# Cross-attention on one core: the rest of A of the last group by block products in one long step, and three pieces of row work on ScalarE

## The chip, the core and the metric

The kernel runs on one core of a Trainium2 chip, in float32. The engines of a core work side by side, each through its own list of instructions in the order written: TensorE (PE, matrix products, with its weight loads PEld), VectorE (DVE), ScalarE (ACT), GpSimd (POOL) and SyncE (SP, which here issues the transfers). They wait for each other by semaphores. The metric is the device time of one execution in microseconds (us): before the change 269.1 us, the median of three runs (268.92 to 269.33).

## The reference

Sixteen batches of 256 rows `x` (256 wide) attend to 77 rows of a context `c` (192 wide) with 8 heads of width 256; then comes a projection, the residual and a layer norm:

```python
Q = (img_embed @ Wq).reshape(B, -1, H, D).transpose(0, 2, 1, 3)
K = (sent_embed @ Wk)...; V = (sent_embed @ Wv)...      # as Q
score = jnp.einsum('bhqd,bhkd->bhqk', Q, K) / math.sqrt(D)
attn = jax.nn.softmax(jnp.where(mask, score, -jnp.inf), axis=-1)
ctx = jnp.einsum('bhqk,bhkd->bqhd', attn, V).reshape(B, -1, H * D)
out = ctx @ Wo + img_embed
mu = jnp.mean(out, axis=-1, keepdims=True)
var = jnp.var(out, axis=-1, keepdims=True)
return (out - mu) * jax.lax.rsqrt(var + EPS) * gamma + beta
```

## The kernel before, in words

**What is computed in which order.** The kernel never forms Q, K or V. For each head it first forms G = Wk'Wq (and U = Wv Wo), from the weights alone. Then A = G'c of a batch (256 x 77 per head) is what the rows of x are multiplied with for the scores, and VW = U'c of a batch is what the attention weights are multiplied with for the output. Batches stand in four groups of four (`GB`); A is held by group in `a_of[g]`, for all 8 heads. Each batch has two tiles of 128 rows, 32 tiles in all; tiles 2b and 2b+1 belong to batch b.

**Two ways to A.** `prepare_a` (L178) forms it directly: for a place (a pair of heads) and two or four batches, 32-column products over 128 rows of c (`part_A`, L203) and over the 64 rows that are left (`part_B`, L215); the results are copied by ACT. `prepare_fast` (L278) forms it for a pair of heads and four batches of a group by 11 block products in place of 12: 64 x 64 products (L361) on sums of blocks of G (`gS`, `gC`) and c (`cT`, `cD`) that were made earlier; ACT copies one block a head (L370), and `put_together` adds the rest on DVE, four additions a head (L373).

**The work on a tile.** `scores` (PE, L469), `shift` (DVE, L486: mask, and the maximum for each head), `exponential` (ACT, L512, eight heads one after the other; with `summed_by_act` ACT also sums each head's row, which costs a read of an accumulator a head, and otherwise DVE sums them in `weigh`, L525), `weigh` (DVE reciprocal L527, POOL multiplication L533), `turn` (DVE transposition L543). Then a batch's output: `seven` (PE, L622: seven block products over both tiles, with sums of the weights `sums` and of VW `differences` made on POOL, and ACT's copy of the products, L647), `add_seven` (DVE L676 and POOL L664, into x), and for the last batches `attend` and `attend_halves` (PE L555, L571). At last the layer norm: `finish` (statistics of the row: by two ACT passes L687 and L688 if `by_act`, otherwise by DVE L691 and L692), `spread` (the reciprocal deviation on ACT, L710 and L711), `normalise` (DVE L731 and L760) and `store` (SP).

**The steps.** The order is written out by hand; each engine takes its instructions in just that order. Batches go in two kinds of steps. A `long_step(b)` takes the scores of batch b+1, `seven(b)`, VW of two batches and two `prepare_fast` calls (one half of a group's heads), and later shifts, turns and normalisations; `short_step(b)`, for the next batch, has only scores, `seven` and what goes with them. They alternate from b = -1 up to `ready`, here 9: long steps at -1, 1, 3, 5 and 7. Work that a step leaves over stands in the list `behind` (the last additions of `put_together`, normalisations) and is done in the next one. From `ready` on come ordinary steps for b = 9 to 14 (the loop before the last lines): scores of b+1, `work_of` of one or two batches (VW, and with it A), exponentials, statistics of batch b-1, `seven(b)` up to b = 12, `attend` after that. In this text "the stage of 9 and 10" is the two steps with b = 9 and b = 10, and so on.

**A of the last group.** Group 3 (batches 12 to 15) gets heads 0 to 3 by `prepare_fast` in the long step of batch 7. Heads 4 to 7 come in the ordinary steps: `work_of` of batches 10, 11, 12 and 13 each adds one `prepare_a` for one pair of heads and two batches, between the products of VW.

**Queues and buffers.** SP issues the loads of x (`load_x`), of its columns (`load_xT`) and the stores, in order. PSUM has eight buffers (`ps_mm`), handed out in turn, which every product's result takes and an ACT or DVE instruction frees.

Of the kernel before, what the change touches and what calls it, by code (L numbers as in the profile page):

```python
# [20 lines left out]
GB = 4  # L21
# [6 lines left out]
def kernel(  # L28
# [14 lines left out]
    B, S, DI = x.shape  # L43
# [3 lines left out]
    NG = B // GB  # L47
    QT = S // P
    NT = B * QT
    GT = GB * QT  # L50
    NF = H // 2
# [40 lines left out]
    def flat(ap):  # L92
        return ap.rearrange("p a b -> p (a b)")
# [10 lines left out]
    NS = B - GB // 2 - 1  # L104
# [23 lines left out]
    def half(i):  # L128
        return slice(i * LB, (i + 1) * LB)
# [21 lines left out]
    def in_two(name, shape, g):  # L151
        return pools[g % 2].tile(shape, F32, tag=f"{name}{g % 2}", name=f"{name}_{g}", bufs=1)
# [25 lines left out]
    def prepare_a(g, places, lo=0, hi=GB, rest_first=False):  # L178


        if 0 in places:
            a_of[g] = in_two("a", [P, 2, GB, H, S2], g)
        parts = [
            (2 * u + i, dc) for u in places for dc in range(2) for i in range(2)
        ]
        batches = slice(g * GB + lo, g * GB + hi)
        each = GB // (hi - lo)
        whole = [
            ps_mm.tile([P, each, hi - lo, S2], F32, tag="mm", name=f"pa_{g}_{h}_{dc}_{lo}")
            for h, dc in parts[: len(parts) // each]  # L190
        ]
        banks = [w[:, i] for i in range(each) for w in whole]
        opening, closing = range(len(whole)), range(len(parts) - len(whole), len(parts))

        def cols(dc, i):
            return slice(dc * P + i * BK, dc * P + (i + 1) * BK)

        wide = 2 if len(places) == 1 and g == 0 else 1

        def part_A():  # L200
            for n, ((h, dc), o) in enumerate(zip(parts, banks)):
                for i in range(NM):
                    nc.tensor.matmul(  # L203
                        flat(o[i * BK : (i + 1) * BK]),
                        gA[:, h, cols(dc, i)],
                        flat(cA[:, batches, :]),
                        start=not rest_first and n in opening,
                        stop=rest_first and n in closing,
                    )

        def part_B():
            for j in range(0, len(parts), 2):
                for i in range(0, NM, wide):
                    for k, (h, dc) in enumerate(parts[j : j + 2]):
                        nc.tensor.matmul(  # L215
                            flat(banks[j + k][i * BK : (i + wide) * BK]),
                            gB[half(k), h // 2, dc * P + i * BK : dc * P + (i + wide) * BK],
                            flat(cB[half(k), batches, :]),
                            start=rest_first and j + k in opening,
                            stop=not rest_first and j + k in closing,  # L220
                        )

        def copies():
            return [(a_of[g][:, dc, lo:hi, h, :], o) for (h, dc), o in zip(parts, banks)]

        return part_A, part_B, copies
# [157 lines left out]
    def prepare_vw(b, rest_first=False):  # L384

        vw_of[b] = vwp.tile([P, 4, 2, P], F32, tag="vw", name=f"vw_{b}", bufs=3)
        parts = slice(0, 4) if b < NS else slice(1, 5)
        pv = [ps_mm.tile([P, 2 * DI], F32, tag="mm", name=f"pv_{b}_{k}") for k in range(2)]

        def part_A():  # L390
            for k in range(2):
                for i in range(NM):
                    nc.tensor.matmul(  # L393
                        pv[k][i * BK : (i + 1) * BK],
                        cA[:, b, k * BK : (k + 1) * BK],
                        uA[:, parts, :, i],
                        start=not rest_first,
                        stop=rest_first,
                    )

        def part_B():
            for i in range(NM):
                for k in range(2):
                    nc.tensor.matmul(  # L404
                        pv[k][i * BK : (i + 1) * BK],
                        cB[half(k), b, k * BK : (k + 1) * BK],
                        uB[half(k), parts, :, i],
                        start=rest_first,
                        stop=not rest_first,
                    )  # L410

        def copies():
            return [
                (vw_of[b][:, :, k, :], pv[k].rearrange("p (q d) -> p q d", q=4)) for k in range(2)
            ]

        return part_A, part_B, copies
# [78 lines left out]
        s_of[t] = s, top  # L496

    def by_act(t):
        return t // QT < B - 2 * GB - 1

    def fast(b):
        return b < B - GB - GB // 2

    def summed_by_act(t):
        return not QT * NS <= t < NT - QT

    def exponential(t):
        s, top = s_of.pop(t)
        den = st.tile([P, H], F32, tag="den", name=f"den_{t}")
        for h in range(H):  # L510
            one = slice(h, h + 1)
            nc.scalar.activation(  # L512
                s[:, h],
                s[:, h],
                AF.Exp,
                bias=top[:, one],
                scale=-1.0,
                accum_out=den[:, one] if summed_by_act(t) else None,
            )
        e_of[t] = s, den  # L520

    def weigh(t):
        e, den = e_of.pop(t)
        if not summed_by_act(t):
            nc.vector.tensor_reduce(den, e, AX.X, ALU.add)  # L525
        rden = st.tile([P, H], F32, tag="rden", name=f"rden_{t}")
        nc.vector.reciprocal(rden, den)  # L527
        p = p_ring[t % 2]
        e_mh = e.rearrange("p (m h) k -> p m h k", h=2)
        rden_mh = rden.rearrange("p (m h) -> p m h", h=2)  # L530
        for cols, keys in ((slice(2 * KM), slice(KM)), (slice(2 * KM, 2 * S2), slice(KM, None))):
            part = p[:, :, cols].rearrange("p m (h k) -> p m h k", h=2)
            nc.gpsimd.tensor_tensor(  # L533
                part,
                e_mh[:, :, :, keys],
                rden_mh.unsqueeze(3).to_broadcast(list(part.shape)),
                ALU.mult,
            )
# [139 lines left out]
    def finish(t):  # L678
        if t in po_of:
            add_product(t)  # L680
        g, j = t // GT, t % GT
        y = x_of(t)[:, 0, :]
        if j == 0:
            mv_of[g] = st.tile([P, GT, 2], F32, tag="mv", name=f"mv_{g}", bufs=2)
        if by_act(t):
            mean, var = (mv_of[g][:, j, n : n + 1] for n in range(2))
            nc.scalar.activation(junk, y, AF.Identity, scale=1.0 / DI, accum_out=mean)  # L687
            nc.scalar.activation(junk, y, AF.Square, bias=mean, scale=-1.0, accum_out=var)  # L688
            return
        bn = st.tile([P, 6], F32, tag="bn", name=f"bn_{t}")  # L690
        nc.vector.bn_stats(bn, y)  # L691
        nc.vector.bn_aggr(mv_of[g][:, j, :], bn)  # L692
# [12 lines left out]
    def spread(first, last):  # L705

        g, lo, hi = first // GT, first % GT, (last - 1) % GT + 1
        log = st.tile([P, GT], F32, tag="log", name=f"log_{first}")
        rstd = st.tile([P, GT], F32, tag="rstd", name=f"rstd_{first}")
        nc.scalar.activation(log[:, lo:hi], mv_of[g][:, lo:hi, 1], AF.Ln, bias=eps, scale=1.0 / DI if by_act(first) else 1.0)  # L710
        nc.scalar.activation(rstd[:, lo:hi], log[:, lo:hi], AF.Exp, scale=-0.5)  # L711
        all_rstd_of[first, last] = rstd
# [424 lines left out]


    def work_of(b, rest_first=False):
        g, n = b // GB + 1, b % GB  # L1140
        work = [prepare_vw(b, rest_first)]
        if b <= NS and not fast(b):
            part = (0, 2) if g < NG else (2, GB)
            work.append(prepare_a(NG - 1, (NF // 2 + n % 2,), *part, rest_first))
        return work

    def copy_out(work):
        for _, _, copies in work:
# [40 lines left out]
    def long_step(b):  # L1189
# [10 lines left out]
        for m in range(0, 2) if b < 0 else range(b + 2, min(b + 3, B // 2)):  # L1200
            turn_last(m)
        works = work_of(b + 1) + work_of(b + 2)
        for part_A, *_ in works:
            part_A()
# [71 lines left out]

        between.append(last_turn)

    ready = B - GB - GB // 2 - 1
    for b in range(-1, ready, 2):  # L1280
        long_step(b)
        short_step(b + 1)
# [2 lines left out]
    for b in range(ready, B - 1):  # L1285
# [6 lines left out]
        g, n = (b + 1) // GB + 1, (b + 1) % GB  # L1292
# [116 lines left out]
```

## Time and profile before

| | before |
|---|---|
| median of 3 runs | 269.1 us (268.92 to 269.33) |
| the profiled execution | 268.58 us, of which the span of the instructions is 266.8 us |
| TensorE busy, granted clock | 260.5 us (98%), 1.00 |
| VectorE / ScalarE / GpSimd busy | 212.7 / 166.9 / 191.5 us (80 / 63 / 72%) |
| last product of TensorE ends | 262.0 us after the start of the span |
| DMA | 22.73 MB, mean 85 GB/s |

Times in the profile are counted from the start of the span of one profiled execution. A row of a group reads: line, engine, operation, what it writes and reads, its shape, how often | busy us, mean ns of one | idle time of the engine before them, and what ended it. A row in order of time reads: start, length, engine, line; an idle time before it stands in brackets with what ended it. A row of waits reads: who waited for whom: us in total, how often, the longest. A row of the chain reads: start, length, what. Matrix products overlap, so the end of a row of PE is later than the next one's start.

### The profile page before, as it was taken

How to read it: one execution, taken by the hardware profiler on the slowest of the kernel's cores; microseconds unless marked ns; L12 is line 12 of the kernel's file. 1: busy time of each engine (PE TensorE's matmuls, PEld its weight loads, DVE VectorE, ACT ScalarE, POOL GpSimd, SP SyncE). 2: the span in 40 equal slices, each digit the busy share in tenths (PEclk: the TensorE clock that was granted, in tenths of full speed). 3: DMA queues.
4: the chain of work that ended last, by engine and by line, in shares of the span. 5: the costliest groups of instructions: out<-in, count | busy, mean ns of one | idle time of the engine just before them, and what ended most of it. 6: DMA issues, size and time to landing. Idle time of an engine off the chain costs nothing.

```text
span 266.8 us, 15067 instructions
## 1 busy us (share of the span) xinstructions
PE 260.5 (98%) x6330; PEld 202.8 (76%) x6330; DVE 212.7 (80%) x860; ACT 166.9 (63%) x710; POOL 191.5 (72%) x272
## 2 busy tenths in 40 slices
PE   7999999999999999999999999999999999999992
PEld 6566578948986899679967996799669957985662
DVE  0554968479893789988997969898988798799785
ACT  3253548624584689648983798467964595636772
POOL 1042098799459896899479996997699899685452
PEclk9999999999999999999999999999999999999999
DMA  6999997900240002131314012221234010100112
GB/s 188 209 206 225 335 148 160 300 18 4 63 104 5 2 6 66 58 90 37 83 43 122 5 24 65 81 85 41 54 127 132 20 44 2 44 23 25 42 43 80
DMA packets 41699, 22.73 MB, mean 85 GB/s; under 512 B 24144, under 2 KB 40608, under 8 KB 41632
## 3 DMA queue, kind: packets, MB, share of 16 engines
q1 hardware_dynamic: 41248, 20.98, 31.3%
q0 software_dynamic: 384, 0.79, 1.3%
q8 instruction: 50, 0.82, 1.3%
q14 instruction: 17, 0.14, 0.2%
HBM read 17.57 MB, written 4.19 MB: 82 GB/s over the span
## 4 chain that ended last, share of the span: by engine, by line
PE 96%; DMA 2%; DVE 1%; SPq 0%; issue 0%; DVEq 0%
PE ps L469 25%; PE pf L361 11%; PE po L622 11%; PE pv L393 10%; PE pm L622 9%; PE pv L404 6%; PE pa L203 5%; PE po L555 4%; PE pu L956 3%; PE pa L215 2%; PE pr L429 2%; PE pgb L1017 2%; DMA wq_nat<-in_L_xattn_Wq_dram 2%; PE pw L970 1%; PE pr L440 1%; PE phb L1033 1%
## 5 line engine op out<-in xcount | busy, mean ns | idle before, releaser
L512 ACT ACTIVATE s<-s,top 128x77 f32<-128x77 f32 x256 | 85.2, 346 | 24.5 <-DVE top L486 24.5
L469 PE MATMUL ps<-a,xT 128*32 128x154 f32 x2048 | 70.1, 294 | 0.0
L469 PEld LDWEIGHTS ps<-a,xT 128*32 128x32 f32 x2048 | 65.8, 110 | 2.0 <-issue 1.5
L533 POOL TENSOR_TENSOR p<-s,rden 128x512 f32<-128x512 f32 x64 | 47.7, 769 | 21.9 <-DVE rden L527 21.7
L486 DVE CUSTOM_DVE_ANT_0 s<-ps,bias 128x77 f32<-128x77 f32 x256 | 43.3, 232 | 4.6 <-PE ps L469 4.0
L512 ACT ACTIVATION_READ_ACCUMULATOR s<-s,top 128x1 f32 x224 | 41.9, 187 | 0.0
L373 DVE TENSOR_TENSOR a<-pf,a 128x154 f32<-128x154 f32 x80 | 33.9, 435 | 7.3 <-PE pf L361 4.9
L664 POOL TENSOR_TENSOR xg<-xg,m 128x256 f32<-128x256 f32 x39 | 28.8, 738 | 2.7 <-DVE xg L676 0.7
L543 DVE STREAM_TRANSPOSE pT<-p 128x640 f32<-128x640 f32 x32 | 26.3, 827 | 5.1 <-POOL p L533 5.0
L393 PE MATMUL pv<-uA,cA 128*32 128x512 f32 x256 | 29.6, 593 | 0.0
L1150 ACT COPY vw<-pv 128x512 f32<-128x512 f32 x32 | 17.1, 587 | 14.9 <-PE pv L404 14.9
L760 DVE SCALAR_TENSOR_TENSOR xg<-xg,rstd,bet 128x256 f32<-128x256 f32 x27 | 22.7, 840 | 2.6 <-ACT rstd L711 1.2
L586 POOL TENSOR_TENSOR ts<-vw 128x768 f32<-128x768 f32 x13 | 23.6, 1831 | 0.0
L486 DVE DVE_READ_ACCUMULATOR2_ANT top<- 128x1 f32 x256 | 20.9, 82 | 0.0
L393 PEld LDWEIGHTS pv<-uA,cA 128*32 128x32 f32 x256 | 8.0, 110 | 13.3 <-issue 9.8
L731 DVE SCALAR_TENSOR_TENSOR xg<-xg,mv,gam 128x256 f32<-128x256 f32 x30 | 18.0, 600 | 0.1
L361 PE MATMUL pf<-cT,gS 64*64 64x154 f32 x240 | 17.4, 290 | 0.0
L603 POOL TENSOR_TENSOR ss<-pT 128x256 f32<-128x256 f32 x13 | 9.7, 745 | 9.8 <-DVE pT L543 9.7
L404 PE MATMUL pv<-uB,cB 64*32 64x512 f32 x256 | 16.3, 596 | 0.0
L622 PE MATMUL po<-vr,pT 128*32 128x256 f32 x208 | 16.0, 379 | 0.0
L361 PEld LDWEIGHTS pf<-cT,gS 64*64 64x64 f32 x240 | 15.8, 133 | 0.0
L203 PE MATMUL pa<-cA,gA 128*32 128x308 f32 (+1 forms) x256 | 14.0, 360 | 0.0
(153 smaller groups left out, 543.1 us busy)
## 6 DMA issues: line engine op xcount, KB each, us to landing
xg<-in_x_dram SPq DMA_DIRECT2D x8, 512.0 KB, 4.4
xT<-in_x_dram SPq DMA_DIRECT2D x56, 64.0 KB, 2.7
out_dram<-xg SPq DMA_DIRECT2D x11, 256.0 KB, 2.7
wo<-in_L_xattn_Wo_dram SPq DMA_DIRECT2D x4, 512.0 KB, 7.9
wq_blk<-in_L_xattn_Wq_dram SPq DMA_DIRECT2D x12, 128.0 KB, 4.6
out_dram<-xg SPq DMA_DIRECT2D x10, 128.0 KB, 1.7
wk_blk<-in_L_xattn_Wk_dram SPq DMA_DIRECT2D x12, 96.0 KB, 4.0
wvT<-in_L_xattn_Wv_dram POOLq DMA_DIRECT2D x8, 96.0 KB, 6.3
```

The lines of the kernel that those rows point to most:

```text
L203: nc.tensor.matmul(flat(o[i * BK : (i + 1) * BK]), gA[:, h, cols(dc, i)], flat(cA[:, batches, :]), start=not rest_first and n in opening, ...
L361: nc.tensor.matmul(bank[half(i), n], weight(i), moving, start=start, stop=stop,)
L373: nc.vector.tensor_tensor(out, *of, ALU.add)
L393: nc.tensor.matmul(pv[k][i * BK : (i + 1) * BK], cA[:, b, k * BK : (k + 1) * BK], uA[:, parts, :, i], start=not rest_first, stop=rest_first,)
L404: nc.tensor.matmul(pv[k][i * BK : (i + 1) * BK], cB[half(k), b, k * BK : (k + 1) * BK], uB[half(k), parts, :, i], start=rest_first, stop=n ...
L469: nc.tensor.matmul(ps[m // 2][i * BK : (i + 1) * BK, m % 2 * 2 * S2 : (m % 2 + 1) * 2 * S2], xT_of[t // PT][:, j * NM + m, dc], flat(a_of[ ...
L486: nc.vector.tensor_tensor_reduce(s[:, h], ps[a][:, k * S2 : (k + 1) * S2], bias[:, b, :], scale=-1.0, scalar=FAR, op0=ALU.add, op1=ALU.min ...
L512: nc.scalar.activation(s[:, h], s[:, h], AF.Exp, bias=top[:, one], scale=-1.0, accum_out=den[:, one] if summed_by_act(t) else None,)
L533: nc.gpsimd.tensor_tensor(part, e_mh[:, :, :, keys], rden_mh.unsqueeze(3).to_broadcast(list(part.shape)), ALU.mult,)
L543: nc.vector.transpose(pT_of[t].rearrange("p n m q -> p m n q"), p.rearrange("p m (n k) -> p m n k", k=BK),)
L622: nc.tensor.matmul(out[i * BK : (i + 1) * BK], weight[:, i], moving, start=first and n == 0, stop=final and n == len(terms) - 1,)
L664: nc.gpsimd.tensor_tensor(to, to, what, ALU.add)
```

## The change

Three lines of conditions and a list are changed, and with them the steps that exist:

- `ready` becomes 11, so that batches 9 and 10 also go by a long step and a short step. The long step of batch 9 calls `prepare_fast` for the pairs of heads 2 and 3 (heads 4 to 7) of group 3, all four batches, 88 products of 64 x 64. The ordinary steps are then b = 11 to 14.
- `work_of` no longer calls `prepare_a`; `fast` is gone. In the ordinary steps b = 9 and b = 11 this removes two calls each.
- `by_act(t)` holds for batches below 9 (before: below 7), so the statistics of batches 7 and 8, four tiles, are two ACT passes a tile in place of DVE's.
- `summed_by_act(t)` leaves out batch 14 alone (before: 13 and 14), so ACT sums the exponentials of batch 13's two tiles.
- The loads of x for batches 14 and 15, which stood in the ordinary step b = 9, now stand in the long step.

```diff
@@ -496,13 +496,10 @@
     def by_act(t):
-        return t // QT < B - 2 * GB - 1
-
-    def fast(b):
-        return b < B - GB - GB // 2
+        return t // QT < B - GB - NF + 1
 
     def summed_by_act(t):
-        return not QT * NS <= t < NT - QT
+        return not QT * (NS + 1) <= t < NT - QT
@@ -1137,12 +1134,7 @@
     def work_of(b, rest_first=False):
-        g, n = b // GB + 1, b % GB
-        work = [prepare_vw(b, rest_first)]
-        if b <= NS and not fast(b):
-            part = (0, 2) if g < NG else (2, GB)
-            work.append(prepare_a(NG - 1, (NF // 2 + n % 2,), *part, rest_first))
-        return work
+        return [prepare_vw(b, rest_first)]
@@ -1276,7 +1268,7 @@
-    ready = B - GB - GB // 2 - 1
+    ready = B - GB - 1
     for b in range(-1, ready, 2):
         long_step(b)
         short_step(b + 1)
```

(`B` = 16, `GB` = 4, `QT` = 2, `NF` = 4, `NS` = 13, `NT` = 32.)

## The prediction

> **What bounds the kernel now.** I read the page first, then the busy time of each engine by stage, then who waits for whom in each stage, and last the order of time on each engine from 185 us on. By the page TensorE (PE) sets the time, and its chain of waits is PE nearly throughout:
>
> ```profile
> PE 260.5 (98%) x6330; PEld 202.8 (76%) x6330; DVE 212.7 (80%) x860; ACT 166.9 (63%) x710; POOL 191.5 (72%) x272
> ...
> PE 96%; DMA 2%; DVE 1%; SPq 0%; issue 0%; DVEq 0%
> ```
>
> By stage (busy time in windows; the columns are the length, then PE, weight load, DVE, ACT, POOL) the last parts are: batches 7 and 8 (a long and a short step), 9 and 10, 11 and 12 (ordinary steps), and the end. PE is busy for the whole of each, so it never stops, but DVE is close behind with 21.5 to 23.6 us:
>
> ```profile
> 157.41:185.00 27.59, 27.59 (x761) 22.66 (x756) 23.64 (x105) 20.70 (x95) 23.55 (x35) 1.00 0.23 64
> 185.00:209.84 24.84, 24.84 (x713) 20.18 (x709) 21.62 (x101) 16.57 (x84) 20.39 (x28) 1.00 0.35 96
> 209.84:234.68 24.84, 24.84 (x713) 20.18 (x708) 21.48 (x97) 15.93 (x68) 22.02 (x28) 1.00 0.07 25
> 234.68:261.90 27.22, 27.22 (x608) 18.11 (x599) 24.17 (x110) 16.63 (x68) 15.78 (x24) 1.00 0.12 39
> ```
>
> Who DVE waits for tells the stages apart. Between 184.9 and 203.3 us it waits once, for POOL, and never for PE:
>
> ```profile
> DVE pT L543 <- POOL p L533: 0.5, 1, 0.5
> ```
>
> From 203.4 to 213.4 us, where batch 10 is masked, exponentiated and turned, its long wait is for ACT:
>
> ```profile
> DVE rden L527 <- ACT s L512: 1.5, 1, 1.5
> DVE s L486 <- PE ps L469: 0.7, 2, 0.3
> ```
>
> And from 238.25 us to the end it waits for PE only 0.5 us:
>
> ```profile
> DVE pT L543 <- POOL p L533: 1.5, 1, 1.5
> DVE xg L676 <- PE po L555: 0.5, 2, 0.3
> ```
>
> So there are two chains beside each other: PE, and one through DVE, ACT (exponentials), POOL (weights, sums) and DVE again. PE sets the time only as long as the second has slack.
>
> **PE, part by part.** The block products of heads 4 to 7 of the last group become two `prepare_fast` calls inside a new long step for batch 9, and the four `prepare_a` calls of batches 10 to 13 go. From the chain in order of time:
>
> ```profile
> 171.01 5.92 PE pf L361 x176
> ...
> 215.92 1.05 PE pa L203 x32
> ...
> 217.99 0.56 PE pa L215 x32
> ...
> 219.41 0.52 PE pa L215 x32
> ...
> 221.79 1.05 PE pa L203 x32
> ```
>
> Added: 5.92 us. Removed: 1.05 + 0.56 + 0.52 + 1.05 = 3.18 us in each of two stages, 6.36. PE gains 0.44. The stages say the same: batches 9 and 10 will take what 7 and 8 take, 27.59 for 24.84 (+2.75), and 11 and 12 take 24.84 - 3.18 = 21.66: together -0.43. A rest of the removed products' switches between 128 and 64 rows may stay; by their dearest spacing the saving is at most 0.3 us away, so PE's part is between -0.7 and -0.1. I take -0.43.
>
> **The other engines' work.** From the groups:
>
> ```profile
> L373 DVE TENSOR_TENSOR a<-pf,a 128x154 f32<-128x154 f32 x80 | 33.9, 435 | 7.3 <-PE pf L361 4.9
> L691 DVE BATCH_NORM_STATS2 bn<-xg 128x6 f32<-128x256 f32 x17 | 7.0, 411 | 0.1
> L525 DVE TENSOR_REDUCE den<-s 128x8 f32<-128x616 f32 x4 | 3.0, 762 | 0.0
> L1150 ACT COPY a<-pa 128x154 f32<-128x154 f32 x16 | 3.5, 306 | 0.2 <-PE pa L203 0.2
> L512 ACT ACTIVATION_READ_ACCUMULATOR s<-s,top 128x1 f32 x224 | 41.9, 187 | 0.0
> ```
>
> DVE gets 16 additions (16 x 0.435 = 7.0 us) and loses four statistics (4 x 0.411 = 1.6, and a little aggregation) and two sums (2 x 0.762 = 1.5): about +3.5 us. ACT loses 16 copies (16 x 0.306 = 4.9 us of pure duration) and gets 16 reads of accumulators, four small copies and two passes for each of four tiles. All of the added DVE and ACT work lies in the new long and short step, where it repeats what batches 7 and 8 do now within 27.59 us with PE never waiting; I cost it there at nothing. If that cover were gone, PE would wait at the next scores for the additions, up to their 7.0 us. The loads of x for batches 14 and 15 move into the long step with their queue order kept (the load, then the two column loads, all on SP), and are used a stage later: nothing. The sums of 13 stretch its exponentials to the pace of batch 11's today, which is the pace used below.
>
> **Where the time goes: the second chain.** The stage of 11 and 12 loses 3.18 us on PE, but nothing of its work on DVE, ACT and POOL lies in the removed products except copies that the chain does not wait for. It starts from the state in which 9 and 10 start now (right after a short step, statistics of the batch before last on DVE, three tiles to normalise), 27.59 us later. So I read its course from 9 and 10 (DVE, ACT, POOL and PE in order of time):
>
> ```profile
> 190.65 0.76 DVE L731 SCALAR_TENSOR_TENSOR xg<-xg,mv,gam 128x256 f32<-128x256 f32 x1
> ...
> 194.39 0.84 DVE L760 SCALAR_TENSOR_TENSOR xg<-xg,rstd,bet 128x256 f32<-128x256 f32 x1
> ...
> 203.38 0.23 DVE L486 CUSTOM_DVE_ANT_0 s<-ps,bias 128x77 f32<-128x77 f32 x1
> ...
> 209.61 0.20 DVE L527 RECIPROCAL rden<-den 128x8 f32<-128x8 f32 x1 [1.48 <-ACT s L512]
> ...
> 213.41 0.22 DVE L486 CUSTOM_DVE_ANT_0 s<-ps,bias 128x77 f32<-128x77 f32 x1
> ...
> 238.25 0.22 DVE L486 CUSTOM_DVE_ANT_0 s<-ps,bias 128x77 f32<-128x77 f32 x1
> ...
> 240.78 0.48 DVE L731 SCALAR_TENSOR_TENSOR xg<-xg,mv,gam 128x256 f32<-128x256 f32 x1
> ```
>
> ```profile
> 203.99 0.36 ACT L512 ACTIVATE s<-s,top 128x77 f32<-128x77 f32 x1 [3.60 <-DVE top L486]
> ...
> 251.80 0.29 ACT L710 ACTIVATE log<-mv,eps 128x2 f32<-128x2 f32 x1 [0.62 <-DVE mv L692]
> ```
>
> DVE reaches the masks of the stage's second batch at 203.38 with no wait for PE; ACT has idled 3.60 us for them and then exponentiates both tiles; DVE's reciprocal of 209.61 waits for ACT; weights, turns and the masks of the next batch (213.41) follow. No link of this is PE, so a shorter PE stage does not shorten it. The masks of batch 14 thus come at 213.41 + 27.59 = 241.00 where they are now at 238.25: **2.75 us later**, while PE is 0.43 earlier. A wait is also added for PE: the products of 12 want a sum (L605) that POOL ends 3.18 us less early relative to PE:
>
> ```profile
> 202.59 0.79 POOL L605 TENSOR_TENSOR ss<-pT,ss 128x256 f32<-128x256 f32 x1
> ```
>
> ```profile
> 206.35 0.62 PE L622 MATMUL pm<-vw,ss 128*32 128x128 f32 x16
> ...
> 259.59 1.06 PE L571 MATMUL po<-vw,pT 128*32 128x128 f32 x32
> ```
>
> Its slack of 206.35 - 203.38 = 2.97 becomes -0.21: PE waits 0.2 us, and behind it the products of 12 and the scores of 14, neither of which the end then waits for.
>
> From 238.25 on DVE is bound by itself, by POOL's weights and, at 251.80, ACT by DVE's statistics. So the delay is handed on, save for the two waits for PE, which it swallows:
>
> ```profile
> 255.52 0.43 DVE L676 TENSOR_TENSOR xg<-po,xg 128x256 f32<-128x256 f32 x1 [0.21 <-PE po L555]
> ...
> 257.07 0.84 DVE L543 STREAM_TRANSPOSE pT<-p 128x640 f32<-128x640 f32 x1
> ...
> 259.84 0.43 DVE L676 TENSOR_TENSOR xg<-po,xg 128x256 f32<-128x256 f32 x1 [0.32 <-PE po L555]
> ...
> 263.51 0.48 DVE L760 SCALAR_TENSOR_TENSOR xg<-xg,rstd,bet 128x256 f32<-128x256 f32 x1
> ```
>
> The last turn ends at 257.91 + 2.75 - 0.21 = 260.45; PE would be ready for it at 259.59 - 0.43 = 259.16, so PE now waits 1.3 us for DVE. That is not what ends last either: DVE's last step comes 2.75 - 0.21 - 0.32 = 2.22 us later than 263.51, and the store behind it with it. **Sum: +2.2 us** on a span of 266.8, that is 269.0; the profiled execution took 268.58, so 270.8. The median of the runs shown, 269.1, lies 0.5 above that execution, so I add to the median: **271.3 us**.
>
> **A price that can move.** The normalisations of 190.65 to 195.23 (three pairs) run beside POOL's additions and cost 4.6 us; the one of 240.78, beside an idle POOL, costs 0.48 for its first half. At that pace three pairs would cost 2.9, 1.7 less. I keep 4.6 because POOL's additions stand at the same place of the order; the bounds of the term are 0 and -1.7, and +0.5 if a quiet pair loses its quiet. The Trainium skill (SBUF — State Buffer, "Who interferes with whom") says that a DVE instruction with two SBUF inputs contends with a GpSimd instruction that reads SBUF, and the second to issue blocks fully. The 0.76 and 0.84 against 0.48 agree; by it the sum falls to +0.5 only if POOL is done with those additions earlier.
>
> **Rivals.** (1) *PE sets the time to the end*: the end comes 0.43 earlier, 268.7 us. For it speak the page's 98% and PE's unbroken stages; against it that DVE has 0.5 us of waits for PE left after 238 and 2.75 to swallow. It decides if DVE reaches batch 14's masks by 238.8, no more than the 0.5 late that those waits hold. This is what the Trainium skill's rule (Trace Analysis, "Identifying the Most-Contended Engine": the one with the highest occupancy is to be optimised first) would suggest; the page's 98% would agree with it. (2) *Partly handed on*: normalisations beside an idle POOL take 1 to 1.5 us off the 2.2: 270.0. (3) *More*: PE's waits move so that the 0.53 is not swallowed and the quiet pairs of the end lose their quiet (+0.5): 271.3 + 1.0 = 272.3.
>
> **How the numbers follow.** This measurement can tell about 0.2%, 0.54 us, from no change. Forecast 271.3 (its own range 270.6 to 271.9): 0.60. Rival 1: 0.18, of which 0.10 within 0.54 us and 0.08 faster. Rival 2: 0.12, slower. Rival 3: 0.10, slower. Slower 0.82, same 0.10, faster 0.08. The range 268.6 to 272.3 takes in rivals 1 and 2 and half of rival 3, and leaves out the faster cases (0.08) and 0.05.
>
> **What would show it.** Right: the fast products near 198 to 204 us with PE unbroken there; the masks of batch 14 near 241.0; an idle time of PE of about 1.3 us before its last group, ended by DVE's turn; a last DVE step near 265.7. Wrong: the masks of batch 14 before 239.5, no idle time on PE before the last products, or a wait of PE already in the new long step.

## The result, and the profile after

The changed kernel takes 271.47 us, the median of six runs (271.09 to 272.95), against 269.1 us before (six runs, 268.92 to 269.34). The ratio is 1.0093, with a 95% interval of 1.0069 to 1.0116: slower by 2.4 us, where 271.3 was forecast. The profiled execution took 271.47 us; its span is 269.3. In the changed kernel the line numbers from `by_act` on are smaller by three, and from `work_of` on by eight: the masks are still L486, but the exponentials are L509, the reciprocal L524, the weights L530, the turn L540, the additions L673, the last half of the normalisation L757, the copy of VW L1142.

The page (busy time of each engine, then the shares of the chain of waits):

```profile
PE 261.6 (97%) x6250; PEld 205.1 (76%) x6250; DVE 214.6 (80%) x866; ACT 170.4 (63%) x730; POOL 191.3 (71%) x272
...
PE 75%; DVE 14%; DMA 3%; POOL 3%; ACT 2%; issue 1%; SPq 1%; DVEq 0%; POOLq 0%; ACTq 0%
```

PE is still busy for 97% of the span, but its share of the chain that ended last is 75%, where it was 96% before. The same chain restricted to the time from 225 us on shows where PE lost it; first the kernel before, then the changed one (shares of that stretch by line):

```profile
by line: PE ps L469 27.9%; PE po L555 24.6%; PE po L622 8.7%; PE pv L393 7.6%; PE po L571 5.0%; PE pv L404 4.5%; PE pm L622 3.9%; DVE xg L731 1.1%; DVE xg L760 1.1%; DVE xg L699 0.7%; DVE bn_halves L700 0.7%; DVE mv L701 0.5%; issue 0.4%; D
```

```profile
by line: POOL p L530 16.9%; ACT s L509 12.3%; DVE s L486 11.0%; DVE pT L540 10.7%; DVE xg L728 9.1%; DVE xg L757 8.6%; DVE xg L673 5.8%; DVE bn L688 4.3%; issue 4.0%; DVE xT L175 2.8%; DVE mv L689 2.1%; DVE den L522 1.5%; DVE rden L524 1.5%
```

The last 44 us of the chain no longer hold a row of PE: weights on POOL, exponentials on ACT, masks, turns and normalisations on DVE follow each other to the end. The windows by stage of the changed kernel (length, then busy time of PE, weight load, DVE, ACT, POOL) are batches 7 and 8, batches 9 and 10, batches 11 and 12, and the end:

```profile
157.62:185.21 27.59, 27.59 (x755) 22.84 (x751) 23.46 (x104) 20.70 (x95) 23.60 (x34) 1.00 0.26 67
185.21:213.03 27.82, 27.82 (x765) 24.80 (x761) 23.82 (x105) 20.57 (x95) 21.60 (x29) 1.00 0.24 64
213.03:234.95 21.92, 21.87 (x584) 16.84 (x580) 20.19 (x95) 12.25 (x61) 18.48 (x25) 1.00 0.17 52
234.95:263.32 28.37, 27.74 (x608) 17.84 (x600) 24.31 (x113) 18.84 (x81) 17.20 (x26) 1.00 0.09 31
```

The new long and short step (batches 9 and 10) costs PE about what batches 7 and 8 cost, and the stage of 11 and 12 is 2.92 us shorter than its 24.84 of before. The end is 1.15 us longer than its 27.22, with 0.63 us in which PE stands. DVE in order of time shows the same from its side: the masks of batch 13, a wait, the reciprocal's wait for ACT, the masks of 14, the last turn and the last step.

```profile
231.38 0.23 DVE L486 CUSTOM_DVE_ANT_0 s<-ps,bias 128x77 f32<-128x77 f32 x1
...
234.69 0.43 DVE L688 BATCH_NORM_STATS2 bn<-xg 128x6 f32<-128x256 f32 x1 [0.70 <-POOL xg L661]
...
237.34 0.20 DVE L524 RECIPROCAL rden<-den 128x8 f32<-128x8 f32 x1 [1.20 <-ACT s L509]
...
241.13 0.22 DVE L486 CUSTOM_DVE_ANT_0 s<-ps,bias 128x77 f32<-128x77 f32 x1
...
258.10 0.37 DVE L673 TENSOR_TENSOR xg<-po,xg 128x256 f32<-128x256 f32 x1
...
259.94 0.84 DVE L540 STREAM_TRANSPOSE pT<-p 128x640 f32<-128x640 f32 x1 [0.26 <-POOL p L530]
...
262.31 0.41 DVE L673 TENSOR_TENSOR xg<-po,xg 128x256 f32<-128x256 f32 x1
...
265.98 0.48 DVE L757 SCALAR_TENSOR_TENSOR xg<-xg,rstd,bet 128x256 f32<-128x256 f32 x1
```

From the masks of 14 to the end DVE now waits for POOL's weights only; the 0.5 us of waits for PE are gone (waits of DVE between 241.13 and 265 us):

```profile
DVE pT L540 <- POOL p L530: 1.8, 2, 1.5
```

To set profiles beside each other, the marks of the table are counted from the first scores of the stage of batches 7 and 8, which the change leaves alone: the row above starts at 157.62 us, that of before at 157.41. "Masks" is the first start of DVE's L486 for that batch, "PE" the end of its last product, "DVE" the end of DVE's last step.

| kernel | first scores at | masks of 13 | masks of 14 | masks of 15 | PE | DVE |
|---|---|---|---|---|---|---|
| before | 157.41 | 70.45 | 80.83 | 90.64 | 104.5 | 106.58 |
| changed | 157.62 | 73.76 | 83.51 | 93.32 | 105.7 | 108.84 |
| changed, second profile (e7) | 157.87 | 73.51 | 83.30 | 93.10 | 105.5 | 108.63 |
| e1, PE's work back | 157.50 | 73.53 | 83.29 | 93.09 | 107.3 | 109.33 |
| e2, before with DVE held up | 157.87 | 70.46 | 84.12 | 93.88 | 106.3 | 109.40 |
| e3, two places of the order | 158.30 | 71.65 | 82.10 | 91.91 | 104.3 | 107.42 |
| e4, without the moved row work | 158.19 | 73.53 | 83.43 | 93.24 | 105.6 | 108.76 |
| e5, the chain's order throughout | 158.05 | 70.66 | 81.41 | 92.20 | 104.6 | 107.74 |
| e8, e5 and less work on DVE | 157.93 | 70.54 | 81.42 | 91.23 | 104.6 | 106.76 |
| e9, only less work on DVE | 158.41 | 78.44 | 89.55 | 99.03 | 111.4 | 114.54 |
| e10, before in the chain's order | 157.93 | 70.69 | 81.71 | 92.51 | 104.9 | 108.02 |
| e11, e9 in another place | 157.64 | 75.64 | 86.95 | 96.42 | 110.2 | 112.21 |

Each line is one execution. The two of the changed kernel differ by 0.2 us at each mark, and timed runs of one kernel lie mostly some tenths of a microsecond and at times more than 1 us apart, so a few tenths in the last column decide nothing; the timed runs below do.

### The profile page after: what moved, and what is told of

Read it like the earlier page. It is cut to its first block, busy times and chain, and to the rows that moved or that the text cites. A ratio compares the mean times of both kernels' runs of the same rounds, so it can differ in the third digit from the quotient of the medians.

```text
span 269.3 us, 14926 instructions
## 1 busy us (share of the span) xinstructions
PE 261.6 (97%) x6250; PEld 205.1 (76%) x6250; DVE 214.6 (80%) x866; ACT 170.4 (63%) x730; POOL 191.3 (71%) x272
## 4 chain that ended last, share of the span: by engine, by line
PE 75%; DVE 14%; DMA 3%; POOL 3%; ACT 2%; issue 1%; SPq 1%; DVEq 0%; POOLq 0%; ACTq 0%
PE ps L469 20%; PE pf L361 13%; PE po L619 9%; PE pv L393 8%; PE pm L619 7%; PE pv L404 4%; POOL p L530 3%; PE pu L953 3%; DVE s L486 3%; PE pa L203 2%; DVE xg L728 2%; DVE xg L757 2%; PE pr L429 2%; DVE pT L540 2%; ACT s L509 2%; PE pgb L1014 2%
## 5 line engine op out<-in xcount | busy, mean ns | idle before, releaser
L509 ACT ACTIVATE s<-s,top 128x77 f32<-128x77 f32 x256 | 86.5, 346 | 20.6 <-DVE top L486 17.1
L530 POOL TENSOR_TENSOR p<-s,rden 128x512 f32<-128x512 f32 x64 | 48.0, 775 | 22.4 <-DVE rden L524 22.2
L373 DVE TENSOR_TENSOR a<-pf,a 128x154 f32<-128x154 f32 x96 | 40.7, 435 | 9.3 <-PE pf L361 6.4
L486 DVE CUSTOM_DVE_ANT_0 s<-ps,bias 128x77 f32<-128x77 f32 x256 | 43.1, 232 | 4.4 <-PE ps L469 4.0
L509 ACT ACTIVATION_READ_ACCUMULATOR s<-s,top 128x1 f32 x240 | 44.9, 187 | 0.0
L540 DVE STREAM_TRANSPOSE pT<-p 128x640 f32<-128x640 f32 x32 | 26.5, 829 | 5.4 <-POOL p L530 5.3
L1142 ACT COPY vw<-pv 128x512 f32<-128x512 f32 x32 | 17.1, 588 | 17.1 <-PE pv L404 17.1
L583 POOL TENSOR_TENSOR ts<-vw 128x768 f32<-128x768 f32 x13 | 23.6, 1829 | 0.0
L757 DVE SCALAR_TENSOR_TENSOR xg<-xg,rstd,bet 128x256 f32<-128x256 f32 x27 | 22.2, 824 | 1.4
L486 DVE DVE_READ_ACCUMULATOR2_ANT top<- 128x1 f32 x256 | 21.0, 82 | 0.0
L361 PE MATMUL pf<-cT,gS 64*64 64x154 f32 x288 | 20.9, 290 | 0.0
L393 PEld LDWEIGHTS pv<-uA,cA 128*32 128x32 f32 x256 | 9.6, 110 | 13.0 <-issue 9.5
L361 PEld LDWEIGHTS pf<-cT,gS 64*64 64x64 f32 x288 | 19.0, 133 | 0.0
L619 PE MATMUL po<-vr,pT 128*32 128x256 f32 x208 | 16.9, 379 | 0.0
L361 PE MATMUL pf<-cB,gB 64*64 64x154 f32 x192 | 16.7, 290 | 0.0
```

The lines of the kernel that those rows point to most:

```text
L361: nc.tensor.matmul(bank[half(i), n], weight(i), moving, start=start, stop=stop,)
L373: nc.vector.tensor_tensor(out, *of, ALU.add)
L393: nc.tensor.matmul(pv[k][i * BK : (i + 1) * BK], cA[:, b, k * BK : (k + 1) * BK], uA[:, parts, :, i], start=not rest_first, stop=rest_first,)
L486: nc.vector.tensor_tensor_reduce(s[:, h], ps[a][:, k * S2 : (k + 1) * S2], bias[:, b, :], scale=-1.0, scalar=FAR, op0=ALU.add, op1=ALU.min ...
L509: nc.scalar.activation(s[:, h], s[:, h], AF.Exp, bias=top[:, one], scale=-1.0, accum_out=den[:, one] if summed_by_act(t) else None,)
L530: nc.gpsimd.tensor_tensor(part, e_mh[:, :, :, keys], rden_mh.unsqueeze(3).to_broadcast(list(part.shape)), ALU.mult,)
```

## The experiments

All were timed in five rounds against the kernel before, on the same chip.

### Is it PE, or the chain beside it? e1 and e2

e1 gives PE the 3.18 us of direct products back, in the stage of 11 and 12 of the changed kernel, and throws their results away; A still comes from the long step.

```diff
     def work_of(b, rest_first=False):
-        return [prepare_vw(b, rest_first)]
+        work = [prepare_vw(b, rest_first)]
+        if b in (NS - 1, NS):
+            part_A, part_B, _ = prepare_a(NG - 1, (NF // 2 + b % GB % 2,), 2, GB, rest_first)
+            work.append((part_A, part_B, lambda: []))
+        return work
```

> The changed kernel with the removed products of batches 12 and 13 (two calls of prepare_a, 3.18 us on PE) made again in the step of batch 11 and thrown away; nothing is added on DVE, ACT or POOL. Theory (the end is set by the chain DVE-ACT-POOL): PE only loses the time for which it now waits, and the time grows by 0.2 to 0.7 us over the changed kernel's 271.5, to 271.7 to 272.2. Rival (PE sets the end, and the new products are dearer than read): all of it is seen, 274.6 us.

Measured: 271.78 us (four runs, 271.62 to 272.15; before on this chip 268.8), ratio 1.011 (1.0093 to 1.0126). The stage of 11 and 12 is back at its old length, and DVE waits for PE again at the end (windows, then the waits of DVE from 238 us on, both of e1):

```profile
185.09:212.68 27.59, 27.59 (x761) 22.68 (x757) 23.60 (x103) 20.59 (x95) 21.58 (x30) 1.00 0.25 66
212.68:237.51 24.83, 24.83 (x712) 20.20 (x707) 21.89 (x101) 15.33 (x77) 20.61 (x28) 1.00 0.15 46
```

```profile
DVE pT L540 <- POOL p L530: 1.5, 1, 1.5
DVE xg L673 <- PE po L552: 0.5, 2, 0.3
```

3.18 us more on PE cost 0.49 us at DVE's end (109.33 against 108.84; 0.70 against the second profile) and 0.3 to 0.4 us in the timed medians. The masks of 14 do not come later for it, 83.29 against 83.51 and 83.30. So the 3.18 us that the change saves on PE in this stage are worth about half a microsecond, since the chain beside PE does not get shorter. In e1 PE's last product ends 2.8 us later than in the kernel before, the masks of 14 come 2.5 later, and the end 2.75 (109.33 - 106.58): there the two chains are again about equally long.

e2 goes the other way: the kernel before, with nothing of the change, and two fills of a dead buffer on DVE ahead of the masks of batch 14.

```diff
+        if b == NS:
+            for _ in range(2):
+                nc.vector.memset(cT.rearrange("p a f k -> p (a f k)")[:, :1512], 0.0)
         scores_and_masks(new, old if b == B - 2 else ())
```

> The kernel before, unchanged but for two fills of a dead tile on DVE (some 2.75 us together) ahead of the masks of batch 14. Theory: a delay of DVE at this place is handed on to the end save for two waits of 0.21 and 0.32 us: 269.1 + 2.2 = 271.3 us (270.8 to 271.8), with no block products moved. Rival (DVE has slack there and PE sets the end): 269.1 us, within 0.5.

Measured: 272.0 us (four runs, 271.81 to 272.17), ratio 1.0116 (1.01 to 1.0132). DVE in order of time in e2:

```profile
239.06 1.32 DVE L1291 MEMSET cT<- 128x1512 f32 x1 [0.27 <-issue]
...
240.75 1.32 DVE L1291 MEMSET cT<- 128x1512 f32 x1 [0.38 <-DVE cT L1291]
...
241.99 0.18 DVE L486 CUSTOM_DVE_ANT_0 s<-ps,bias 128x77 f32<-128x77 f32 x1
...
266.78 0.48 DVE L760 SCALAR_TENSOR_TENSOR xg<-xg,rstd,bet 128x256 f32<-128x256 f32 x1
```

The time is 0.2 us above my range, as with the gaps the fills took more than the 2.75 meant: the masks of 14 come 3.29 us later (84.12 against 80.83) and the end 2.82 later (109.40 against 106.58). What is swallowed, 0.47, is nearly the 0.53 of DVE's two waits for PE, and these waits are gone from e2's trace. Only DVE was touched here, in a kernel whose chain of waits is 96% PE; a delay of this size on it reaches the end by itself. The two runs together name the second chain: in the changed kernel 3.18 us of PE work are nearly free, and in the kernel before 3.29 us of DVE's time are not.

### Is it the row work that moved to ScalarE? e4

```diff
     def by_act(t):
-        return t // QT < B - GB - NF + 1
+        return t // QT < B - 2 * GB - 1
     def summed_by_act(t):
-        return not QT * (NS + 1) <= t < NT - QT
+        return not QT * NS <= t < NT - QT
```

> The changed kernel with the conditions of the row work as before: statistics of batches 7 and 8 and sums of 13 back on DVE; only the products and the steps are changed. Theory (the loss is the shorter PE stage of 11 and 12 against an unchanged chain): 271.5 us, within 0.6, as the statistics lie in the long step where DVE has 1.5 us of idle time before the new additions. Rival (the three pieces moved to ScalarE cost the time): back to 269.1 us, within 0.5.

Measured: 270.95 us (five runs, 270.81 to 271.52), ratio 1.0079 (1.0062 to 1.0096). The interval overlaps the changed kernel's and the marks lie within 0.1 us of it at the masks of 14 and at the end. The slowdown comes with the products; the statistics and sums on ScalarE do not cause it, and no help from them can be measured.

### The change again: e7

The changed kernel itself, run beside e5.

> The changed kernel as it is, beside the two kernels with other orders on the same chip: 271.5 us (271.1 to 271.9), as measured. A rival that puts the loss on the chip or on the moment would see less than half of it, under 270.3.

Measured: 271.37 us (four runs, 271.27 to 271.9), ratio 1.0093 (1.0078 to 1.0109), the same as the first time.

### Can the chain be shortened where it has lost its cover? e3 and e5

If the order of DVE's list sets the course of the stage of 11 and 12, changing the order alone must give time back. e3 changes two places of the order in the step of batch 11: the turn and the additions left over from the step before go ahead of the masks of 12, where they stood between them, so that POOL gets its sums earlier; and the normalisation of batch 10's second tile goes behind the masks of 13.

```diff
     statistics(tiles_of(ready - 2))
+    while between:
+        between.pop(0)()
...
-            if alone or ahead:
+            if ahead and g == NG:
+                turn_some_x(g, n)
+                behind.append(partial(normalise, old[1]))
+            elif alone or ahead:
                 turn_x_and_normalise(g, n, old)
```

> The changed kernel with two orders changed in the step of batch 11 and no work added or taken away: the second turn of batch 11 (and the sums and additions behind it) is issued ahead of the masks of batch 12, so that POOL starts its sums some 1.3 us earlier, and the normalisation of tile 21 goes behind the masks of batch 13, so that they start 1.65 us earlier. Theory (the chain through POOL and DVE in this stage sets the end): the masks of batch 14 come about 2.5 us earlier and the time falls by about 2.2 us to 269.2 (268.8 to 269.9), where PE bounds it again. Rival (PE's new products or a lower clock cost the time): 271.5 us, no change.

Measured: 270.2 us (five runs, 270.08 to 270.66), ratio 1.0051 (1.0036 to 1.0066). With the same work on every engine this gives back 1.1 to 1.3 us of the loss, less than the 2.2 I had expected. DVE in order of time in e3:

```profile
229.95 0.22 DVE L486 CUSTOM_DVE_ANT_0 s<-ps,bias 128x77 f32<-128x77 f32 x1
...
234.99 0.43 DVE L688 BATCH_NORM_STATS2 bn<-xg 128x6 f32<-128x256 f32 x1 [1.43 <-POOL xg L661]
...
240.40 0.22 DVE L486 CUSTOM_DVE_ANT_0 s<-ps,bias 128x77 f32<-128x77 f32 x1
```

The masks of 13 come 2.1 us earlier than in the changed kernel (71.65 against 73.76), those of 14 only 1.4. In between stand the statistics of batch 11, which now wait 1.43 us for POOL (0.70 in the changed kernel), and the reciprocal of the second tile stands behind them. The end follows the masks of 14: 1.42 earlier.

e5 keeps e3's first edit and takes out that wait as well: the statistics of old batches go behind both tiles' weights, one of the three waiting normalisations goes behind the first weights, and the later normalisations behind the next masks.

```diff
-        while behind:
+        while len(behind) > (b == ready):
             behind.pop(0)()
...
             exponential(t)
-            finish(old[i])
+            if b >= NS:
+                finish(old[i])
             weigh(t)
+            while behind:
+                behind.pop(0)()
+        for t in old if b < NS else ():
+            finish(t)
...
-            normalise(old[0])
             for t in new:
                 turn(t)
-            if alone or ahead:
-                turn_x_and_normalise(g, n, old)
...
+            turn_some_x(g, n)
+            behind.extend(partial(normalise, t) for t in old)
```

> The changed kernel with the order of the steps of batches 11 and 12 written for the chain, no work added or taken away: the second turn of batch 11 ahead of the masks of batch 12, one of three waiting normalisations behind the first weights, the weights ahead of the statistics of the batch before, and both normalisations of a batch behind the next masks, so that the turns come first. In the kernel with two of these orders changed the reciprocal of tile 26 still stood behind statistics that waited 1.43 us for POOL's additions. Theory: with that gone too the masks of batch 14 come 2 us earlier than there, DVE has slack again, and PE bounds the end: 268.8 us on the scale of 269.1 for the kernel before (268.4 to 269.5), and PE has no idle time after 213 us. Rival (the rest of the loss, some 1.4 us, is not the chain's): 270.2 us, as there.

Measured: 269.87 us (five runs, 269.73 to 270.85; before 269.01), ratio 1.004 (1.0026 to 1.0053), hardly apart from e3 and above my range. The masks of 13 are back where the kernel before has them (70.66) and those of 14 come 0.7 earlier than in e3, but those of 15 come 0.3 later (92.20 against 91.91). In order of time, the masks of 14 and of 15 in e5:

```profile
239.46 0.22 DVE L486 CUSTOM_DVE_ANT_0 s<-ps,bias 128x77 f32<-128x77 f32 x1
...
250.25 0.22 DVE L486 CUSTOM_DVE_ANT_0 s<-ps,bias 128x77 f32<-128x77 f32 x1
```

From one to the other are 10.79 us; in the kernel before, and in the changed one, 9.81. Between 239.4 and 254 us DVE waits for nobody in e5. The normalisation that was put behind the masks of 14 costs its whole length there. PE, meanwhile, is what I had expected: it waits for nothing after 213 us. The windows of e5 for the stage of 11 and 12 and the end are

```profile
213.74:235.40 21.66, 21.66 (x585) 16.90 (x580) 20.34 (x97) 14.82 (x74) 18.77 (x26) 1.00 0.14 40
235.40:262.68 27.28, 27.27 (x608) 18.07 (x599) 23.62 (x111) 16.69 (x67) 16.25 (x25) 1.00 0.14 47
```

PE's last product stands where the kernel before has it (104.6 for 104.5), and only DVE's end is later, by 1.16 us (107.74 against 106.58). So the order is worth something up to batch 14, and from there on it is the amount of DVE's work that sets the time.

### The same order in the kernel before: e10

The edits of e5 in the kernel before, save that all waiting normalisations stay ahead of the weights. With that edit too (e6) the program deadlocks and has no time. I put it down to the load of x for batches 14 and 15, which here stands in this step and must wait for a store behind it; no run shows that this is the cause.

> The kernel before with the orders of the chain kernel in its steps of batches 9 to 12 (all three waiting normalisations ahead of the first weights, as the load of x for batches 14 and 15 waits for their stores). Theory: PE bounds it already, so an earlier chain is worth nothing: 269.0 us (268.6 to 269.4). Rival (the orders are a gain of their own, whatever bounds the end): 268.0 us or less.

Measured: 270.41 us (six runs, 269.96 to 270.65; before 269.14), ratio 1.0049 (1.0035 to 1.0063). I had expected no loss, and it is 1.3 us. The masks of 14 come 0.9 later and those of 15 another 1.0 (92.51 against 90.64). Between these masks stand two normalisations where before stood one; in order of time in e10 they are

```profile
242.17 0.48 DVE L731 SCALAR_TENSOR_TENSOR xg<-xg,mv,gam 128x256 f32<-128x256 f32 x1
242.75 0.48 DVE L760 SCALAR_TENSOR_TENSOR xg<-xg,rstd,bet 128x256 f32<-128x256 f32 x1
243.16 0.48 DVE L731 SCALAR_TENSOR_TENSOR xg<-xg,mv,gam 128x256 f32<-128x256 f32 x1
243.67 0.48 DVE L760 SCALAR_TENSOR_TENSOR xg<-xg,rstd,bet 128x256 f32<-128x256 f32 x1
```

and the second, from 243.16 to 244.15, is the 1.0 us. The order is no improvement in itself: it moves DVE work out of the stage of 11 and 12, where the kernel before has PE to cover it, into a stretch without slack.

### Less work for DVE: e8, e9 and e11

e8 adds to e5 what its reading asks for: the statistics of four more tiles (batches 10 and 11) and the sums of batch 14's two tiles go to ACT, which in the changed kernel idles 5.14 us for the masks of 13:

```profile
231.71 0.36 ACT L509 ACTIVATE s<-s,top 128x77 f32<-128x77 f32 x1 [5.14 <-DVE top L486]
```

The edit beside e5's:

```diff
     def by_act(t):
-        return t // QT < B - GB - NF + 1
+        return t // QT < B - GB - NF + 1 or t // QT in (NS - 3, NS - 2)
     def summed_by_act(t):
-        return not QT * (NS + 1) <= t < NT - QT
+        return True
```

> The kernel with the order of the steps of batches 11 and 12 written for the chain, and besides some 3.9 us taken from DVE after batch 10: the statistics of batches 10 and 11 (four tiles) and the sums of batch 14 (two tiles) go to ScalarE. With the orders alone the masks of batch 14 came 1.2 us earlier than with two orders and the end only 0.2, with DVE never waiting from 239 to 254 us. Theory (what ends last is all of DVE's work left after batch 10, more than one link of the chain): PE bounds the end and the time is 268.6 us on the scale of 269.0 for the kernel before (268.2 to 269.2). Rival (something else of the changed kernel keeps 0.9 us): 269.9 us, no change by the relief.

Measured: 268.65 us (twelve runs, 268.31 to 269.26) against 269.14 of before (seventeen runs): ratio 0.9987 (0.9977 to 0.9997). This beats the changed kernel by 2.8 us. It beats the kernel before by 0.5 us in the medians and by 0.35 by the ratio, whose interval goes from 0.1 to 0.6 us. DVE's busy time on the page falls from 213.6 us in e5 to 209.9; the windows of e8 for the stage of 11 and 12 and the end are

```profile
213.61:235.27 21.66, 21.66 (x584) 16.90 (x580) 19.55 (x92) 17.56 (x86) 18.77 (x26) 1.00 0.14 40
235.27:262.55 27.28, 27.28 (x608) 18.12 (x600) 22.08 (x108) 19.89 (x92) 16.68 (x25) 1.00 0.14 47
```

As in e5, PE is unbroken, the stage takes the 21.66 us that its products add up to, and the end is as short as before (27.22). PE's last product stands at the same mark as in e5, 104.6, so what DVE's end gains, 0.98 us (106.76 against 107.74), comes from the relief of DVE. The gain over the kernel before is about what PE saves by the change, 0.43. It rests on the timed runs: the profiled execution was the slowest of the twelve (269.26 us), with 27.86 and 27.82 us for the two stages ahead that take 27.59 in e1, and its marks do not show it.

e9 is the same relief without the order of e5, in the changed kernel.

> The changed kernel in its own order with only the relief of DVE: the statistics of batches 10 and 11 and the sums of batch 14 on ScalarE. Theory (DVE's work left after batch 10 sets the end): 1.5 to 2.5 us of the loss come back, 269.4 us (268.9 to 270.2). Rival (only the order of the chain through POOL in the step of batch 11 matters): 271.4 us, within 0.4.

Measured: 276.84 us (five runs, 276.42 to 277.51), ratio 1.0283 (1.0266 to 1.0301). ACT in order of time in e9:

```profile
224.08 0.42 ACT L684 ACTIVATE last_rows<-xg 128x256 f32<-128x256 f32 x1 [5.00 <-POOL xg L661]
```

I missed by seven microseconds. The trace shows one large reason: in the written order a row's statistics stand between the exponentials of the step's two tiles. On DVE they delayed little; on ACT they wait 5.00 us for POOL's additions to x, and the exponentials of the second tile wait behind them, and so do its weights, turn and the masks of the next batch (78.44, 4.7 later than in the changed kernel).

e11 puts ACT's statistics behind both tiles' weights, and changes nothing else against e9.

```diff
             exponential(t)
-            finish(old[i])
+            if not by_act(old[i]):
+                finish(old[i])
             weigh(t)
+        for t in old:
+            if by_act(t):
+                finish(t)
```

> The changed kernel with the statistics of batches 10 and 11 and the sums of batch 14 on ScalarE, where ScalarE's two passes for a batch now stand behind the exponentials of both new tiles (in the run before they stood between them, and the second tile's exponentials waited 5.0 us for POOL's additions). Every other order is the changed kernel's. Theory: without that wait the relief of DVE is worth what DVE has left to do after the masks of batch 14, some 1.5 us: 269.9 us (269.4 to 270.6), between the changed kernel and the kernel with order and relief. Rival (the loss of the run before was the weight of the added ScalarE work itself, not its place): 275 us or more.

Measured: 274.43 us (five runs, 274.05 to 274.96; before 268.87), ratio 1.0209 (1.0195 to 1.0223). This is 2.0 (by the ratios) to 2.4 us (by the medians) less than e9, but nearer to the rival than to my range. The waits of DVE in e11 between 222 and 244.6 us:

```profile
DVE rden L524 <- ACT s L509: 3.1, 2, 2.5
DVE xg L757 <- ACT rstd L708: 2.9, 2, 1.7
DVE xg L728 <- ACT last_rows L685: 1.7, 2, 0.9
```

The wait has in part moved on: the normalisation of batch 10 stands ahead of the turns on DVE, and it now waits for the mean and the deviation that ACT makes so late. DVE's reciprocals wait for ACT besides. The added ACT work by itself is not the loss, as e8 has the same work and is the fastest. In e8, where the normalisations have gone behind the next masks, DVE waits for neither the mean nor the deviation. So in the changed kernel the relief needs the order and the order needs the relief; each alone is slower than the kernel before.

## Why the prediction was right, and where it was off

**PE's part, -0.43: right as work, and not what sets the end.** The fast products took

```profile
199.05 5.93 PE pf L361 x176
```

for the 5.92 taken. The stage of 9 and 10 was 27.82 us in this profile, for 27.59; the stage of 11 and 12 took 21.92 for 21.66. e3's profile has both as forecast, 27.59 and 21.66. e1 shows how little of the saving in the stage of 11 and 12 reaches the end.

**The added work at nothing: right.** DVE's additions, the copies and the statistics by ACT lie in the new long and short step without a wait of PE there, and e4 bears out that the moved row work changes nothing that can be measured. DVE's busy time grew by 1.9 us (212.7 to 214.6), where the prediction added up 3.5; nothing in the sum hung on it. (Its "21.5 to 23.6 us" for DVE by stage leaves out the 24.17 of its last row.)

**The wait of PE for POOL's sum, 0.2: right.** In order of time, the two kinds of products of batch 12 in the changed kernel, the sum that the second kind waits for on POOL, and the same products in the kernel before:

```profile
230.78 0.62 PE L619 MATMUL pm<-vw,pT 128*32 128x128 f32 x16
...
231.44 0.65 PE L619 MATMUL pm<-vw,ss 128*32 128x128 f32 x16
```

```profile
230.59 0.80 POOL L602 TENSOR_TENSOR ss<-pT,ss 128x256 f32<-128x256 f32 x1
```

```profile
230.76 0.62 PE L622 MATMUL pm<-vw,pT 128*32 128x128 f32 x16
231.19 0.62 PE L622 MATMUL pm<-vw,ss 128*32 128x128 f32 x16
```

They start 0.66 us apart, where the same two stand 0.43 apart in the kernel before and 0.44 in e8 (231.35 and 231.79): 0.22. POOL ends that sum at 230.59 + 0.80 = 231.39.

**The second chain, +2.75 at the masks of 14: right, with two small errors of opposite sign.** It is 2.68 by the marks (83.51 against 80.83). But the masks of 13 came 3.3 us later (73.76 against 70.45), where the course of batches 9 and 10 gives 3.1 (203.38 + 27.59 against 227.87), and the way from there to the masks of 14 took 9.75 us, where that course gives 10.03. In the second profile of the changed kernel it is 3.1 and 9.79, and 2.47 in all; so the first error is within the scatter, the second is not, and that 2.68 lies so near to 2.75 is in part luck. Three waits account for the shorter way. The statistics wait 0.70 us for POOL, which the course of 9 and 10 does not show; the reciprocal waits 1.20 us for ACT and not 1.48; and the two waits of 0.33 us for PE's scores, which stand at the masks in that course, are gone. So the prediction's "No link of this is PE" was not quite so: its own rows show those 0.7 us.

**Handed on save for the two waits for PE, +2.22: right.** DVE's end came 2.26 later (108.84 against 106.58). The two waits for PE are gone. A new one of 0.26 us at the last turn, for weights that took POOL 1.64 us, came in. That makes 2.68 - 0.53 + 0.26 = 2.41, and the profiles do not tell where the other 0.15 went. The second profile of the changed kernel gives 2.05. e2 shows the same handing on with nothing of the change in it.

**The price kept at 4.6: right.** The three pairs of normalisations run again beside POOL's additions, from the first to the last of these rows of the changed kernel:

```profile
218.68 0.77 DVE L728 SCALAR_TENSOR_TENSOR xg<-xg,mv,gam 128x256 f32<-128x256 f32 x1
...
222.44 0.84 DVE L757 SCALAR_TENSOR_TENSOR xg<-xg,rstd,bet 128x256 f32<-128x256 f32 x1
```

that is 223.28 - 218.68 = 4.60 us. The contention that the Trainium skill describes (SBUF — State Buffer, "Who interferes with whom") agrees in direction; five of the six rows take 0.68 to 0.95 us, against 0.48 beside an idle POOL, and one takes 0.49.

**PE's idle time ahead of its last products: wrong.** The step "PE now waits 1.3 us for DVE", ahead of the last group and ended by DVE's turn, failed. PE in order of time in the changed kernel, and the copy on ACT that it waited for:

```profile
258.47 1.98 PE L552 MATMUL po<-vw,pT 128*32 128x256 f32 x32 [0.58 <-ACT vw L1142]
...
260.93 1.08 PE L568 MATMUL po<-vw,pT 128*32 128x128 f32 x32
```

```profile
257.86 1.04 ACT L1142 COPY vw<-pv 128x512 f32<-128x512 f32 x2
```

PE waits 0.58 us, one group earlier, for VW of batch 15. ACT has this copy behind the exponentials of batch 15, and these were late with the masks. The prediction had followed the delay on DVE and POOL alone and had not asked what else is queued behind a late engine. The last turn did end about where forecast (260.78; 260.45 and the 0.21 by which this profile starts its stages later make 260.66), and the last group starts 0.15 us behind it; but PE was busy until then with products that its own wait had made late, so the 1.3 us never appeared. The second profile of the changed kernel has the same wait for VW (0.6 us). The price for the end was nothing, as DVE did not wait for those products.

**The rivals.** *PE sets the time to the end* falls by e1 and e2. *Partly handed on* falls with the 4.60 us. *More* would have needed DVE's two waits for PE to stay; they are gone. That the last microseconds are bound by DVE's amount of work, and not by the place of one instruction, the prediction had said in part, of the time after 238 us; e5 and e8 bear it out.

What stays open is how e8's gain over the kernel before divides between PE's saving and the relief of DVE: the order and the relief were not tried together in the kernel before.

## What to carry to other kernels

Where PE is busy throughout, look for a second chain beside it and measure its slack stage by stage, by which of its waits are ended by PE: products moved to an earlier stage take cover away from the other engines' work in the stage that they leave. Before row work goes to an engine that idles, see what stands behind it in that engine's list and when its input comes, and what stands behind its result on the engine it left. An order that helps one kernel can hurt the next by as much (here e5 and e10), because it only moves work to where another stretch has slack or has none.

## What the runs showed that was not expected

A fill of 128 x 1512 elements took DVE 1.32 us, and DVE stood 0.27 and 0.38 us ahead of the two. The statistics of four tiles and the sums of two, moved from DVE to ACT, made the changed kernel 5.4 us slower at one place of the list (276.84 against 271.4), and at another, in e8, they went with the fastest version of all.
